# Loading the sorted rows of the expert blocks: two blocks' rows per block in place of a whole stage's rows at once

## The chip, the cores and the metric

One core of a Trainium2 chip runs the kernel. The metric is the device time of one execution in microseconds (us), taken as the median of several runs. A profile of one more execution gives what each engine did and when: PE (TensorE, the matrix products), ACT (ScalarE), DVE (VectorE), POOL (GpSimd), and SP (SyncE), which here does nothing but issue transfers (DMAs).

## The reference

32 sequences of 128 tokens of width 128 pass through gated cross-attention and then through a gated mixture of experts. All in float32. Cut to its core:

```
x = x + tanh(g_xattn) * cross_attention(layernorm(x), ctx)     # 16 heads of 64, 128 keys each
n = layernorm(x)                                               # 4096 tokens x 128
scores = sigmoid(n @ gate_w.T)                                 # 32 experts in 4 groups of 8
group score = sum of the two best (scores + bias) of a group; the best 2 groups stay
the 8 best experts within these two groups; their scores, normalized to 2.5, are the weights w
routed = sum over the 8 experts of w * (silu(n @ gate_e) * (n @ up_e)) @ down_e    # inner size 64
shared = (silu(n @ sg) * (n @ su)) @ sd
out = x + tanh(g_ffn) * (routed + shared)
```

A token only ever needs the experts of its two groups. There are six pairs of groups.

## The kernel before

**Attention.** A loop over the 32 sequences (lines 931 to 1009) holds the attention. It ends some 310 us into the profiled span, and it is the same in both kernels.

**Sorting.** The tokens are dealt into six classes, one for each pair of groups, and written row by row into a table `xs` in DRAM, so that 128 rows in succession are a *block* whose tokens share their pair of groups. A row holds the token's 16 expert weights, its 128 normalized values and its number. This happens in three batches (`choose`, line 513), since the first tokens are through the attention long before the last. Each batch makes a set of blocks known: 7, then 8, then 22 (`SHARE`, line 49), which the code calls stages 0, 1 and 2. Of the 37 blocks, 35 are always worked on (`NSURE`), the last two only if the data need them (line 1350). POOL writes the rows with indirect DMAs (`put`, line 698). When the table of a stage is computed, `ready[k]` is set; `complete(k)` (line 1250) also asks that no row of the stage is still to be written.

**Blocks.** The loop at line 1309 goes over the blocks j. For each of the two groups s of a block, PE multiplies the block's tokens with the gate and up weights of 8 experts (`g` and `u`, 128x512 each), ACT takes the silu of `g` (tile `act`), DVE multiplies `u` by the expert weights (tile `uw`), then `act` by `uw` (tile `h`). PE multiplies `h` with the down weights, and both groups add into `y`. ACT scales it to `o`, and POOL adds `o` to the output rows with an indirect DMA (`finish`, line 1223). Work is issued one half-block ahead: in iteration j stand, in this order, `gate_up(j+1, 0)`, `down(j, 0)`, `gate_up(j+1, 1)` and `down(j, 1)`. `g` and `u` each have two buffers in PSUM, so the product `u` of one half-block can start only once DVE has read `u` of two half-blocks before.

**Two forms of a block.** In a *narrow* block the tokens are on the partitions (`gate_up`, line 1128), and the expert weights are columns of the loaded rows themselves. In a *wide* block (`gate_up_wide`, line 1193) the hidden units are on the partitions, so that `h` needs no turning before the down product; the expert weights of each token must then lie along the free axis, repeated on every partition. That takes a detour over DRAM, begun three blocks ahead:

- `turn_weights` (line 1165): PE turns the block's weights, ACT copies them to `wq` (line 1170) and the tokens to `xT`, and SP stores `wq` to DRAM as `wr` (line 1174).
- `spread_weights` (line 1176): SP loads `wr` back twice, each time repeated on 64 partitions, into the tile `wb` (line 1179). DVE reads `wb` in line 1205.

`wide(j)` (line 1161) holds for blocks 10 to 14 and 17 to 34. Blocks 15 and 16 are narrow.

**Loads of rows.** `load(j)` (line 1098) reads the block's place in `xs` from a table into a register of SP and issues the DMA `xb<-xs` (line 1107), 128 rows of 145 floats. The tile `xb` has 16 buffers. `more_loads(must, may)` (line 1253) is called at the start of every iteration j. It issues all loads up to block `must` (some two or three blocks ahead), and beyond that every load up to block `may` = j + 13 whose stage is complete:

```
more_loads(j + AHEAD if j + AHEAD < NSURE and wide(j + AHEAD) else j + 2, j + 13)
```

**What sets the order.** The order of the work is written out by hand (`tc.manual_schedule()`): each engine, SP among them, takes its instructions in the order of the code. SP's queue thus holds the loads of iteration j ahead of the store and the loads of `wb` that the end of iteration j issues. A DMA that has to wait holds back every later one of SP. When SP has issued eight DMAs, the ninth waits until the first of them has landed, since eight semaphores are used in turn.

Of the kernel before, what the change touches and what calls it, by code (L numbers as in the profile page):

```python
# [39 lines left out]
NSURE = NBLK - 2  # L40
# [14 lines left out]
def gated_cross_attention_moe(  # L55
# [422 lines left out]
    def turn2(pt, c, n):  # L478
        for k in range(n):
            nc.tensor.transpose(pt[:, k * P : (k + 1) * P], rows[:, c + k, NEP:RID], ident)  # L480

    def turned2_out(pt, c, n):
        nc.scalar.copy(x2T[:, c * P : (c + n) * P], pt)

    def logits(pl, c, n):
        for k in range(n):
            nc.tensor.matmul(
                pl[:, k * E : (k + 1) * E], x2T[:, (c + k) * P : (c + k + 1) * P], gw_sb,
                start=True, stop=True,
            )  # L490
# [4 lines left out]
    def logits_out(pl, c, n):  # L495

        k = max(i for i in range(3) if first[i] <= c)
        d = scs[k][:, c - first[k] : c - first[k] + n, :]
        nc.scalar.activation(d, pl.rearrange("p (i e) -> p i e", e=E), AF.Exp, scale=-1.0)

    def logits_done(c, n):
        k = max(i for i in range(3) if first[i] <= c)
        d = scs[k][:, c - first[k] : c - first[k] + n, :]
        v.tensor_scalar(d, d, 1.0, None, ALU.add)
        v.reciprocal(d, d)
# [303 lines left out]
    def gap(room, transfers=1):  # L809

        fresh = True
        while batches and 3 - len(batches) < opened:
            if not piece:
                step_on()
                continue
            w = piece[0]
            if w == "n":
                if not fresh:
                    break
                step_on()  # L820
            elif w in ("pe", "act"):
                break
            else:
                if room <= 0:
                    break
                room -= w
                step_on()
            fresh = False
        put_rows(transfers)
# [6 lines left out]
    def up_products(t, g, u):  # L836
        x_ = x2T[:, t * TT : (t + 1) * TT]
        nc.tensor.matmul(g, sg_sb, x_, start=True, stop=True)
        nc.tensor.matmul(u, su_sb, x_, start=True, stop=True)

    def gated(g, u, a, h):
        nc.scalar.activation(a, g, AF.Silu)
        v.tensor_tensor(h, a, u, ALU.mult)

    def down_products(y, h):
        for i in range(TB):
            nc.tensor.matmul(y[:, i, :], h[:, i * P : (i + 1) * P], sd_sb, start=True, stop=True)
# [3 lines left out]
    def base_out(t, y, o):  # L851
        v.scalar_tensor_tensor(
            out=o, in0=y, scalar=tg2, in1=x_all[:, t * TB : (t + 1) * TB, :],
            op0=ALU.mult, op1=ALU.add,
        )
        w = nc.sync.dma_start(
            out=out_rows[t * TT : (t + 1) * TT, :].rearrange("(i p) d -> p i d", p=P), in_=o
        )
        bases.append(w.ins.name)
# [215 lines left out]
    def small_psum(name):  # L1075
        return ps_t.tile([P, TT], F32, tag="t", name=name)
# [14 lines left out]
    def stage(j):  # L1091
        return max(i for i in range(3) if sum(SHARE[:i]) <= j)

    def psum_place(name):
        place("pe", small_psum(name) if piece and piece[0] == "pe" else None)
        place("act")

    def load(j):
        while not ready[stage(j)]:
            if not piece or piece[0] not in ("pe", "act"):  # L1100
                step_on()
            psum_place(f"pr_{j}")
        while pending and pending[0][0] <= stage(j):
            put_rows(1)
        row, = loaded(mybir.EngineType.SP, j, 0, 1, NROWS - P)
        xbs[j] = m16.tile([P, RW], F32, tag="xb", name=f"xb_{j}")
        reads = [nc.sync.dma_start(out=xbs[j], in_=xs[bass.ds(row, P), :])]
        for r in reads:
            for name in sorts:
                tc.add_manual_dep(  # L1110
                    r.ins, name,
                    mybir.DependencyInfo(mybir.DependencyClass.Sync, mybir.DependencyReason.DATA),
                    reason="the sorted rows",
                )

    def number(j):

        idx[j] = m16.tile([P, 1], I32, tag="idx", name=f"idx_{j}")
        v.tensor_scalar(idx[j], xbs[j][:, RID:], -1.0, float(B * P), ALU.mult, ALU.add)

    def xprep(j):
        pt = small_psum(f"px_{j}")[:, 0:P]
        nc.tensor.transpose(pt, xbs[j][:, NEP:RID], ident)
        xTs[j] = m3.tile([P, P], F32, tag="xT", name=f"xT_{j}")
        nc.scalar.copy(xTs[j], pt)
        groups[j] = loaded(mybir.EngineType.PE, j, 1, 3, NG - 1)
# [34 lines left out]
    def wide(j):  # L1161
        at = j - (NBLK - SHARE[2])
        return -5 <= at < 0 or at >= 2
# [80 lines left out]

    AHEAD = 3
    loaded_ = [0]

    def complete(k):  # L1250
        return ready[k] and not (pending and pending[0][0] <= k)

    def more_loads(must, may):
        while loaded_[0] < NSURE and (
            loaded_[0] <= must or (loaded_[0] <= may and complete(stage(loaded_[0])))
        ):
            load(loaded_[0])
            loaded_[0] += 1

    with tc.manual_schedule():  # L1260
        more_loads(AHEAD, AHEAD)
        hsh = {}

        def up(t):
            g = ps_g.tile([P, TT], F32, tag="g", name=f"sg_{t}")
            u = ps_g.tile([P, TT], F32, tag="u", name=f"su_{t}")
            up_products(t, g, u)
            a = m3.tile([P, TT], F32, tag="act", name=f"sa_{t}")
            hsh[t] = m4.tile([P, TT], F32, tag="h", name=f"sh_{t}")
            gated(g, u, a, hsh[t])  # L1270

        def down_base(t):
            y = ps_y.tile([P, TB, D], F32, tag="y", name=f"sy_{t}")
            down_products(y, hsh.pop(t))
            base_out(t, y, m4.tile([P, TB, D], F32, tag="so", name=f"so_{t}"))

        up(4)
        up(5)
        gap(1.2, 2)
        down_base(4)  # L1280
        psum_place("prs_4")
        gap(1.2, 2)
        up(6)
        pt = small_psum("pt2")
        turn2(pt, 28, 4)
        turned2_out(pt, 28, 4)
        down_base(5)
        gap(1.2, 2)
        pl = small_psum("pl2")[:, 0 : 8 * E]
        logits(pl, 24, 8)  # L1290
        logits_out(pl, 24, 8)
        psum_place("prs_5")
        logits_done(24, 8)
        up(7)
        gap(1.2, 2)
        xprep(0)
        down_base(6)
        psum_place("prs_6")
        gap(1.2, 2)
        opened = 3  # L1300
        gate_up(0, 0)
        xprep(1)
        down_base(7)
        gate_up(0, 1)
        for j in range(AHEAD + 1):
            number(j)
        turned_hidden(0, 0)
        done = -1
        for j in range(NSURE):
            more = j + 1 < NSURE  # L1310
            more_loads(j + AHEAD if j + AHEAD < NSURE and wide(j + AHEAD) else j + 2, j + 13)
            if more:
                (gate_up_wide if wide(j + 1) else gate_up)(j + 1, 0)
            if j + 2 < NSURE and wide(j + 2):
                place_weights(j + 2, 0)
            if done < j - 1:
                finish(j - 1)
                if j - 1 + AHEAD < NSURE:
                    number(j - 1 + AHEAD)
            down(j, 0)  # L1320
            if not wide(j):
                turned_hidden(j, 1)
            if j + 2 < NSURE and not wide(j + 2):
                xprep(j + 2)
            psum_place(f"prb_{j}")
            gap(1.4, 1)
            if more:
                (gate_up_wide if wide(j + 1) else gate_up)(j + 1, 1)
            if j + 2 < NSURE and wide(j + 2):
                place_weights(j + 2, 1)  # L1330
            down(j, 1)
            if not wide(j) or not more:
                finish(j)
                done = j
                if AHEAD < j + AHEAD < NSURE:
                    number(j + AHEAD)
            if more and not wide(j + 1):
                turned_hidden(j + 1, 0)
            if j + AHEAD < NSURE and wide(j + AHEAD):
                turn_weights(j + AHEAD)  # L1340
                spread_weights(j + AHEAD)
            gap(1.4, 2)
# [71 lines left out]
```

## Time and profile before

| | us |
|---|---|
| median of 3 runs | 552.41 (552.32 to 552.97) |
| the profiled execution's own time | 552.61 |
| its span, first to last instruction | 550.8 |
| PE busy | 512.7 (93% of the span) |
| DVE busy | 406.0 (74%) |
| ACT busy | 380.5 (69%) |
| POOL busy | 275.2 (50%) |
| mean granted clock of PE | 0.982 of full speed |

The span is what the trace shows; the own time of the same execution also holds 1.8 us around it. The chain that ended last (the profile follows it back from the last instruction, at each step to what released it) runs 71% over PE, 19% over DVE, 3% over ACT and 2% over DMAs. In a timeline line, the first two numbers are the start and the length of a piece of work in us. A line of the waits gives who waited for what, the sum in us, how many times, and the longest one.

### The profile page before, as it was taken

The numbers are of one execution on the slowest core, as the hardware profiler recorded it, in microseconds if no ns is written. First come the engines' busy times: TensorE is split into PE (matmuls) and PEld (weight loads), VectorE is DVE, ScalarE is ACT, GpSimd is POOL, SyncE is SP. The second block draws the span as 40 slices with busy tenths as digits, with TensorE's granted clock in tenths as the row PEclk, the third lists the DMA queues.
The fourth block names the chain that finished last, engine by engine and source line by source line (L and its number), as shares of the span: only waits on it lengthen the run. The fifth ranks groups of instructions, "written<-read, shape, count | busy, mean of one in ns | idle before, by whom it ended". The sixth has DMA issues, their size and how long they took to land.

```text
span 550.8 us, 15971 instructions
## 1 busy us (share of the span) xinstructions
PE 512.7 (93%) x5942; PEld 448.1 (81%) x5942; DVE 406.0 (74%) x920; ACT 380.5 (69%) x1422; POOL 275.2 (50%) x248
## 2 busy tenths in 40 slices
PE   5899999999999999998999979999996999999992
PEld 4777888988999988897977656676895799999992
DVE  3779999898998899998887877998652455555551
ACT  1688989989899888997882234444772577777760
POOL 5355557566775756864764811743752212232332
PEclk9899999999999999999999979999999999999997
DMA  9994440806213010000001332131555255453541
GB/s 238 226 336 145 151 150 14 289 4 202 99 34 138 2 42 1 2 2 3 2 2 31 97 95 41 38 70 16 122 132 107 51 117 122 104 123 85 129 89 15
DMA packets 50524, 50.49 MB, mean 92 GB/s; under 512 B 20992, under 2 KB 39168, under 8 KB 50064
## 3 DMA queue, kind: packets, MB, share of 16 engines
q1 hardware_dynamic: 43968, 44.38, 28.0%
q0 software_dynamic: 6192, 4.56, 5.8%
q8 instruction: 49, 0.80, 0.6%
q10 hardware_dynamic: 288, 0.52, 0.3%
q14 instruction: 27, 0.22, 0.2%
HBM read 28.06 MB, written 21.58 MB: 90 GB/s over the span
## 4 chain that ended last, share of the span: by engine, by line
PE 71%; DVE 19%; ACT 3%; POOL 2%; DMA 2%; issue 1%; POOLq 0%; SPq 0%; DVEq 0%
PE y L1216 11%; PE o_ps L436 8%; PE s_ps L369 8%; PE g L1199 7%; PE u L1199 7%; PE o_ps L415 7%; PE o_ps L328 6%; DVE nmax L376 5%; DVE eT L404 4%; PE u L1133 4%; PE g L1131 4%; DVE xn L307 3%; PE ph L1152 2%; ACT e L389 2%; DVE oT L424 1%
## 5 line engine op out<-in xcount | busy, mean ns | idle before, releaser
L389 ACT ACTIVATE e<-s_ps,nmax 128x128 f32<-128x128 f32 x512 | 181.6, 384 | 9.6 <-DVE nmax L376 8.2
L398 POOL TENSOR_TENSOR e<-e,rs 128x1024 f32<-128x1024 f32 x64 | 121.4, 1898 | 92.5 <-DVE rs L396 92.5
L1227 POOL DMA_INDIRECT out_dram<-o,idx x35 | 55.8, 1594 | 133.6 <-ACT o L1225 102.8
L389 ACT ACTIVATION_READ_ACCUMULATOR e<-s_ps,nmax 128x1 f32 x512 | 114.0, 223 | 0.0
L376 DVE TENSOR_REDUCE nmax<-s_ps 128x8 f32<-128x1024 f32 x64 | 76.9, 1202 | 11.7 <-PE s_ps L369 11.5
L1205 DVE TENSOR_TENSOR uw<-u,wb 128x512 f32<-128x512 f32 x46 | 31.8, 691 | 67.6 <-PE u L1199 53.7
L404 DVE STREAM_TRANSPOSE eT<-e 128x1024 f32<-128x1024 f32 x64 | 78.7, 1229 | 0.9 <-POOL e L398 0.9
L369 PEld LDWEIGHTS s_ps<-kvT_sb,qT 64*128 64x128 f32 x1024 | 63.8, 191 | 18.7 <-issue 11.1
L369 PE MATMUL s_ps<-kvT_sb,qT 64*128 64x128 f32 x1024 | 76.1, 289 | 3.0 <-ACT e L389 1.9
L436 PE MATMUL o_ps<-c_sb,oT 128*128 128x128 f32 x512 | 65.4, 281 | 6.8 <-DVE oT L424 6.8
L436 PEld LDWEIGHTS o_ps<-c_sb,oT 128*128 128x128 f32 x512 | 59.7, 191 | 13.6 <-DVE oT L424 10.7
L415 PE MATMUL o_ps<-eT,kv 32*64 32x256 f32 x2048 | 66.0, 380 | 2.1 <-DVE c_sb L285 1.0
L328 PE MATMUL o_ps<-xnT,a_sb 128*128 128x128 f32 x480 | 59.8, 278 | 0.0
L328 PEld LDWEIGHTS o_ps<-xnT,a_sb 128*128 128x128 f32 x480 | 56.6, 194 | 0.3 <-issue 0.2
L415 PEld LDWEIGHTS o_ps<-eT,kv 32*64 32x64 f32 x2048 | 49.4, 131 | 8.1 <-DVE c_sb L285 1.4
L1216 PE MATMUL y<-ed_sb,h 128*128 x368 | 49.0, 277 | 0.0
L1199 PE MATMUL u<-xT,wc 128*128 128x128 f32 x368 | 48.6, 275 | 0.0
L1199 PE MATMUL g<-xT,wc 128*128 128x128 f32 x368 | 48.6, 275 | 0.0
L1216 PEld LDWEIGHTS y<-ed_sb,h 128*128 128x128 f32 x368 | 45.6, 195 | 1.5 <-issue 1.0
L1203 ACT ACTIVATE act<-g 128x512 f32<-128x512 f32 x46 | 27.5, 597 | 27.0 <-PE g L1199 27.0
L1199 PEld LDWEIGHTS u<-xT,wc 128*128 128x128 f32 x368 | 44.8, 192 | 0.0
L1199 PEld LDWEIGHTS g<-xT,wc 128*128 128x128 f32 x368 | 44.7, 192 | 0.0
(203 smaller groups left out, 813.7 us busy)
## 6 DMA issues: line engine op xcount, KB each, us to landing
xs<-zero SPq DMA_DIRECT2D x8, 1740.0 KB, 10.3
wb<-wr SPq DMA_DIRECT2D x46, 256.0 KB, 3.7
kv<-in_kv_dram SPq DMA_DIRECT2D x32, 128.0 KB, 4.9
xb<-xs SPq DMA_DIRECT2D x35, 72.5 KB, 2.4
x_all<-in_x_dram SPq DMA_DIRECT2D x8, 256.0 KB
kvT_sb<-in_kvT_dram SPq DMA_DIRECT2D x6, 256.0 KB, 6.0
eg_sb<-in_exp_gT_dram SPq DMA_DIRECT2D x1, 1024.0 KB, 6.9
eu_sb<-in_exp_uT_dram SPq DMA_DIRECT2D x1, 1024.0 KB
```

The source lines that it names most:

```text
L328: nc.tensor.matmul(o_ps[1][:, p // HP, p % HP * P : (p % HP + 1) * P], a_sb[:, p].rearrange("d j k -> d (j k)"), x_, start=True, stop=True,)
L369: nc.tensor.matmul(s_ps[g][:, j, q, :], qT[b][r, g * HP + q, :], kvT_sb[r, b * P : (b + 1) * P], start=True, stop=True,)
L376: v.tensor_reduce(nmax[b, g], s_ps[g].rearrange("p j q k -> p (j q) k"), AX.X, ALU.max, negate=True)
L389: nc.scalar.activation(es[b][:, g, j, q, :], s_ps[g][:, j, q, :], AF.Exp, bias=n[:, c], accum_out=sums[b, g][:, c],)
L398: nc.gpsimd.tensor_tensor(e, e, rs.unsqueeze(2).to_broadcast([P, NP, P]), ALU.mult)
L404: v.transpose(eTs[b][:, g].rearrange("p j q n -> p (j q n)"), es[b][:, g].rearrange("p j q n -> p (j q n)"))
L415: nc.tensor.matmul(o_ps[a // 2][j * KV : (j + 1) * KV, a % 2, 0 : NP * Q].rearrange("k (g q n) -> k g q n", g=2, q=HP), kv_sb[b // TB][r, ...
L436: nc.tensor.matmul(o_ps[0][:, 0, 0:D], o[:, p].rearrange("k a n -> k (a n)"), c_sb[:, p, :], start=(p == 0), stop=(p == NP - 1),)
L1199: nc.tensor.matmul(pt[:, q, :], w[:, k, q * P : (q + 1) * P], xTs[j], start=True, stop=True)
L1205: v.tensor_tensor(uw, u, wbs[j][:, s], ALU.mult)
L1216: nc.tensor.matmul(ys[j], hT[:, q, :], ed_all[:, bass.ds(groups[j][s] * FG + q * D, D)], start=(s == 0 and q == 0), stop=(s == 1 and q == ...
L1227: w = nc.gpsimd.indirect_dma_start(out=out_rows, out_offset=bass.IndirectOffsetOnAxis(ap=idx.pop(j), axis=0), in_=o, in_offset=None, bound ...
```

## The change

`more_loads` gets a third argument `most`: the number of loads that one call may issue while it is ahead of `must`. Loads that `must` asks for are issued as before, but count too. In the loop over the blocks `most` is 2. The call ahead of the loop, which has `must` and `may` both at 3, gets 0.

```
-    def more_loads(must, may):
+    def more_loads(must, may, most):
         while loaded_[0] < NSURE and (
-            loaded_[0] <= must or (loaded_[0] <= may and complete(stage(loaded_[0])))
+            loaded_[0] <= must or (most > 0 and loaded_[0] <= may and complete(stage(loaded_[0])))
         ):
             load(loaded_[0])
             loaded_[0] += 1
+            most -= 1
...
-        more_loads(AHEAD, AHEAD)
+        more_loads(AHEAD, AHEAD, 0)
...
-            more_loads(j + AHEAD if j + AHEAD < NSURE and wide(j + AHEAD) else j + 2, j + 13)
+            more_loads(j + AHEAD if j + AHEAD < NSURE and wide(j + AHEAD) else j + 2, j + 13, 2)
```

## The prediction, made before the result was known

> **What bounds the kernel now.** I read the waits of the whole span first, then the timelines of SP, DVE and PE around the longest wait that reaches PE, then the table of stretches with the granted clock. The waits (who, for what: us in total, times, longest):
>
> ```profile
> DVE uw L1205 <- PE u L1199: 53.7, 42, 1.8
> ...
> DVE uw L1205 <- DMA wb<-wr: 13.9, 3, 10.1
> ...
> PE u L1133 <- DVE uw L1205: 5.2, 1, 5.2
> ```
>
> Most of DVE's waits here are for PE, which is the later of the two. Three times DVE waits for `wb` instead, once for 10.1 us, and once PE then waits for DVE. The waits of PE from 426 us to the end name this one alone. The three stretches from 429 to 540 us show PE busy without a gap, at the full clock; here is one:
>
> ```profile
> 429.00:465.00 36.00, 36.00 (x291) 33.02 (x291) 17.29 (x32) 25.68 (x57) 7.79 (x6) 1.00 0.43 97
> ```
>
> So PE bounds the kernel from 429 us on: what PE gains at 425 us reaches the end, what others gain later does not. Why was `wb` late? SP's timeline:
>
> ```profile
> 403.51 0.31 SPq L1174 DMA_DIRECT2D wr<-wq  x1
> 406.26 1.08 SPq L1179 DMA_DIRECT2D wb<-wr  x2
> 409.11 8.87 SPq L1107 DMA_DIRECT2D xb<-xs  x10
> 418.07 0.38 SPq L1174 DMA_DIRECT2D wr<-wq  x1
> 420.26 1.10 SPq L1179 DMA_DIRECT2D wb<-wr  x2
> 421.92 2.07 SPq L1107 DMA_DIRECT2D xb<-xs  x3
> ```
>
> The ten loads of blocks 15 to 24, stage 2's first burst, stand ahead of block 14's store `wr`. ACT had written its `wq` at 408.81 + 0.26 = 409.07 us (ACT's timeline), yet it goes out at 418.07. DVE and PE pay:
>
> ```profile
> 414.07 0.69 DVE L1207 TENSOR_TENSOR h<-act,uw 128x512 f32<-128x512 f32 x1
> 424.90 0.69 DVE L1205 TENSOR_TENSOR uw<-u,wb 128x512 f32<-128x512 f32 x1 [10.14 <-DMA wb<-wr]
> ```
>
> ```profile
> 414.86 1.06 PE L1199 MATMUL u<-xT,wc 128*128 128x128 f32 x8
> ...
> 419.44 1.02 PE L1131 MATMUL g<-eg_sb,xT 128*128 x2
> 425.65 2.07 PE L1133 MATMUL u<-eu_sb,xT 128*128 x2 [5.19 <-DVE uw L1205]
> 427.52 1.68 PE L1216 MATMUL y<-ed_sb,h 128*128 x8
> 429.03 0.27 PE L1123 MATMUL px<-ident,xb 128*128 128x128 f32 x1
> ```
>
> Block 15's `u` needs the buffer that block 14's `uw` still has to read. After the pause PE is slow for a while:
>
> ```profile
> 425.65:429.10 3.45, 3.45 (x11) 2.41 (x12) 3.19 (x6) 0.00 (x0) 0.00 (x0) 0.54 0.00 1
> ```
>
> The last three numbers are clock, DMA share and GB/s: 0.54 of the full clock.
>
> **What the change moves.** It adds and removes no instruction. I compared the two built programs queue by queue: PE, ACT, DVE and POOL keep the order of their work, and only the semaphores of some DMA waits are renumbered. On SP three things follow.
>
> *Start and stage 1.* Blocks 0 to 14 are loaded in the same order, and nothing stands between the loads of 7 to 14 in either program, so spreading them over four iterations of the code changes nothing: the first `wr` (block 10) comes behind load 14 both times. Cost 0, up to 409 us.
>
> *The burst.* Between the `wb` of block 13 and the `wr` of block 14 there are two loads (15, 16) instead of ten. One load costs SP (8.87 - 0.33) / 9 = 0.95 us. Eight fewer: 7.6 us. `wr` goes out at 418.07 - 7.58 = 410.49 us, and its `wq` is there (409.07). From `wr` to `wb` it took 2.19 us (420.26 - 418.07), and 1.39 (433.15 to 434.54) to 2.75 (403.51 to 406.26) elsewhere; I take 2.19, the same transfer behind the same kind of loads: 412.68. From the issue of `wb` to `uw` it took 4.64 us (424.90 - 420.26); the waits for blocks 12 and 13 ended 4.99 and 4.88 us after theirs (400.39 to 405.38, 406.26 to 411.14), and the shortest landing, 3.4, on the second of the pair, 0.63 later, gives 4.03. I take 4.64: `uw` starts at 417.3, bounds 415.96 to 418.2. (415.96 is when `u` itself is there: 414.86 + 1.10, as in 439.61 to 440.71.)
>
> When would this hold PE? Without the pause block 15's `u` follows its `g` by 0.86 us (429.14 to 430.00): 420.30. `uw` takes 0.69 and the handover 0.06, so `uw` must start by 419.55. The next reader, `y` of block 14 at 421.16, needs `h`, 1.49 us behind the start of `uw`: by 419.67. I have 2.2 us to spare, and 1.3 at the late bound. PE's pause goes; DVE still waits some 1.3 us for `wb`, and that is the next late thing, hidden behind PE.
>
> The sum on PE: start of `u` 425.65 - 420.30 = 5.35; that `u` took 427.52 - 425.65 = 1.87 instead of 0.86, so 1.01; the `y` behind it 429.03 - 427.52 = 1.51 instead of 0.89, so 0.62. Together **6.98 us**.
>
> *The loads that were eight earlier.* Loads 17 to 22 come behind `wb` of block 14, in iterations 12 to 14, where no `wr` stands between: about 414 to 419.5 us, while the next `wr` (block 17) has its `wq` only at 433.1 - 7.0 = 426.1. Cost 0. Then the `wr` of blocks 18 to 22 each have two loads ahead instead of one. In a steady iteration now: `wr` 450.79, `wb` 452.21, load 453.87 + 0.34 = 454.21, next `wr` 456.37. One more load (0.95) ends at 455.16, so 1.2 us stay free; the first of these iterations, with narrow halves, is longer still (433.15 to 439.46). Cost 0. If that cover were gone, `wb` has more: its pair lands by 452.21 + 0.63 + 4.2 (the longest landing) = 457.0, `uw` of that block starts at 457.88, and PE itself would wait only if `uw` were another 4.2 us late (block 17: `uw` 440.71 + 0.75, block 18's `u` 445.63). The rows still arrive blocks ahead: block 17's by 417 us, and they are turned only in iteration 14. The 16 buffers that loads 17 on take were last read in blocks 1 on. POOL's output DMAs follow `o`, which follows PE.
>
> **The sum.** The profiled execution took 552.61 us: 552.61 - 6.98 = 545.63. The median of the runs is 0.20 lower: **545.4 us**, 1.3% less. A difference under 0.2% (1.1 us) cannot be told from no change here.
>
> **The rivals.**
>
> *Part of the pause stays (0.08).* `wr` and `wb` of block 14 now run beside POOL's output DMAs of 412.03 and 416.19 and the loads 15 to 18. Each us by which the two legs exceed 6.83 + 2.2 = 9.1 us is a us of PE. Against it: the longest legs seen sum to 2.75 + 4.99 = 7.7. With 2 us of pause: 547.4. A pause of 3.5 us that brings the slow clock back gives 545.4 + 3.5 + 1.63 = 550.5. (The Trainium skill, "TensorE: Matmul & The Clock Gate", Part 1, says that PE falls to half clock after an idle window of about 3.4 us. By that rule the 2 us pause would cost no clock; no shorter pause in this stage shows it.)
>
> *No gain (0.04).* If moving the issues moved nothing, because `wb` waits for the transfers and not for SP, the time stays 552.4. The row speaks against it: `wr` went out 0.09 us after the tenth load was issued (409.11 + 8.87 = 417.98), not after it landed, which takes 2.4 us more. (The skill, "DMA: Bandwidth & Descriptors", "Issuing engines are not separate DMA queues", calls the time to initiate a DMA usually small relative to the DMA itself. By that rule there would be little to gain; ten issues in 8.87 us with `wr` right behind say otherwise.) That the change does not do what it says belongs here; SP's new order speaks against it.
>
> *Slower (0.05).* Five times (`wr` of blocks 18 to 22) a second load stands ahead of `wr`. It decides if such a load costs SP L > 1.2 + 0.95 = 2.15 us, as it would if it waited for an earlier transfer. Lateness then adds up to 5 x (L - 2.15), of which 0.9 + 4.2 = 5.1 us are covered. If a load waits out the longest landing of one (4.0) and its own 0.95, L is 4.95: 5 x 2.8 - 5.1 = 8.9 us on PE, 545.4 + 8.9 = 554.3. It is slower from L = 4.8 on. Against it: the last three loads of the burst behind `wb` (421.92, 2.07 us for three) wait for nothing.
>
> **How the numbers follow.** Forecast 0.83, the others as given. The range takes the forecast with the spread of the runs (0.65 us downward: 544.7) and the small part of the partial pause (up to 2 us: 547.5). Faster: 0.83 + 0.08 = 0.91; within 0.2%: 0.04; slower: 0.05.
>
> **What would show it.** Right: SP issues two loads, then `wr` near 410.5 and `wb` near 412.7; `uw` waits for `wb` 1 to 3 us instead of 10.1; PE has no wait for `uw` in line 1133 and no stretch near 0.54 clock; the span is 543.8. Wrong: a wait of PE for `uw` in blocks 15 to 23, `uw` waiting for `wb` in blocks 18 to 22, or SP held at line 1107 between two `wb`.

## The result, and the profile after

| | before | after |
|---|---|---|
| median | 552.69 us (552.32 to 555.17, 4 runs) | 544.48 us (543.8 to 547.05, 4 runs) |
| ratio | | 0.9851, 95% interval 0.9807 to 0.9894 |
| the profiled execution's own time | 552.61 | 544.62 |
| its span | 550.8 | 542.8 |
| mean granted clock of PE | 0.982 | 0.987 |

The change is faster by 8.2 us. The forecast was 545.4; the median lies 0.2 us below the lower end of the range (544.7). First the waits of the kernel after (who, for what: us in total, times, longest):

```profile
DVE uw L1205 <- PE u L1199: 38.5, 31, 1.8
...
DVE uw L1205 <- DMA wb<-wr: 23.6, 10, 4.4
```

The longest wait of `uw` for `wb` is 4.4 us instead of 10.1, and PE's wait for `uw` in line 1133 is not in the list any more. There are, however, ten waits for `wb` instead of three; the section on the experiments comes back to them. SP's timeline shows the new order:

```profile
404.84 1.08 SPq L1179 DMA_DIRECT2D wb<-wr  x2
409.34 1.91 SPq L1107 DMA_DIRECT2D xb<-xs  x2
411.31 0.42 SPq L1174 DMA_DIRECT2D wr<-wq  x1
413.08 1.09 SPq L1179 DMA_DIRECT2D wb<-wr  x2
414.70 5.22 SPq L1107 DMA_DIRECT2D xb<-xs  x6
```

Two loads, then the store of block 14 at 411.31 instead of 418.07; loads 17 to 22 follow behind its `wb`. On DVE and on PE:

```profile
418.14 0.69 DVE L1205 TENSOR_TENSOR uw<-u,wb 128x512 f32<-128x512 f32 x1 [4.37 <-DMA wb<-wr]
```

```profile
418.44 1.02 PE L1131 MATMUL g<-eg_sb,xT 128*128 x2
419.30 1.02 PE L1133 MATMUL u<-eu_sb,xT 128*128 x2
420.16 1.05 PE L1216 MATMUL y<-ed_sb,h 128*128 x8
421.05 0.27 PE L1123 MATMUL px<-ident,xb 128*128 128x128 f32 x1
```

`u` follows `g` by 0.86 us, and `y` and `px` come at their full-speed distances. From this `g` to this `px` it took 2.61 us; before it took 9.59 (419.44 to 429.03). The difference is 6.98 us, the sum of the prediction to the last digit: the sum was read from this same profile before, and what remained to be seen was that nothing of the pause stays. But `g` itself starts 1.00 us earlier than before, and nothing that the change moves lies ahead of it. In this pair of profiles that microsecond fits the granted clock 90 us earlier, after PE's pause at 320 us, where it waits for the first row loads: there the kernel after is still 0.47 us later than before (323.60 against 323.13, the first product of block 0), and on the way to `g` it wins back 1.5, with 3.4 us less at half clock (at most 1.7 us of work). In the stretches from 320 to 325 us and from 325 to 330 us (third number from the end: clock) the kernel before shows

```profile
320.00:325.00 5.00, 1.94 (x7) 1.29 (x7) 3.51 (x16) 1.20 (x3) 0.00 (x0) 0.80 0.26 60
325.00:330.00 5.00, 5.00 (x14) 2.83 (x14) 2.98 (x14) 0.86 (x2) 0.00 (x0) 0.52 0.56 159
```

and the kernel after

```profile
320.00:325.00 5.00, 1.89 (x7) 0.93 (x6) 4.09 (x17) 1.77 (x3) 0.00 (x0) 0.91 0.25 59
325.00:330.00 5.00, 5.00 (x21) 3.44 (x21) 3.28 (x15) 0.86 (x2) 0.00 (x0) 0.75 0.62 172
```

At half clock a stretch of 5 us with a mean of 0.80 has 2.0 us of it and one with 0.52 has 4.8: 6.8 us before, and 0.9 + 2.5 = 3.4 us after. From 330 us on the clock is 1.00 in both. So there is one theory for each part: for the 7 us the place of `wr` and `wb` in SP's queue, against the traffic of ten loads at once; for the remaining microsecond luck of the clock, against an effect of the change that the prediction did not see.

### The profile page after: what moved, and what is told of

Its sections match the earlier page's. It is cut to its first block, busy times and chain, and to the rows that moved or that the text cites. A ratio compares the mean times of both kernels' runs of the same rounds, so it can differ in the third digit from the quotient of the medians.

```text
span 542.8 us, 15971 instructions
## 1 busy us (share of the span) xinstructions
PE 509.8 (94%) x5942; PEld 447.1 (82%) x5942; DVE 405.7 (75%) x920; ACT 380.5 (70%) x1422; POOL 275.6 (51%) x248
## 4 chain that ended last, share of the span: by engine, by line
PE 72%; DVE 20%; ACT 3%; POOL 2%; issue 1%; DMA 1%; POOLq 0%; DVEq 0%
PE y L1216 11%; PE o_ps L436 8%; PE u L1199 8%; PE g L1199 8%; PE s_ps L369 8%; PE o_ps L415 7%; PE o_ps L328 6%; DVE nmax L376 5%; DVE eT L404 4%; PE g L1131 4%; PE u L1133 4%; DVE xn L307 3%; PE ph L1152 2%; ACT e L389 2%; DVE oT L424 1%
## 5 line engine op out<-in xcount | busy, mean ns | idle before, releaser
L1227 POOL DMA_INDIRECT out_dram<-o,idx x35 | 56.2, 1607 | 124.7 <-ACT o L1225 91.2
```

What stands on the lines that cost most here:

```text
L1227: w = nc.gpsimd.indirect_dma_start(out=out_rows, out_offset=bass.IndirectOffsetOnAxis(ap=idx.pop(j), axis=0), in_=o, in_offset=None, bound ...
```

## The experiments

Since the time ahead of block 15 differs between executions, I read each trace by its *tail*, the span less the start of the first `g` of block 15 (419.44 before, 418.44 after). *Lead* is the time from the issue of load 15 to that `g`, *reach* the time from the issue of load 15 to `uw` of block 14. The pause is what the start of `u` loses against 0.86 us behind `g`. All in us; the last column is the ratio to the kernel before on the same chip with its 95% interval.

| kernel, loads ahead of `wr` | reach | lead | pause | tail | ratio |
|---|---|---|---|---|---|
| before, 10 | 15.79 | 10.33 | 5.35 | 131.4 | |
| before again, 10 | 15.45 | 11.38 | 3.96 | 130.2 | 1.0026 (0.9999 to 1.0053) |
| eight per block, 8 | 13.50 | 11.32 | 2.07 | 126.8 | 0.9939 (0.9911 to 0.9967) |
| six per block, 6 | 11.52 | 11.34 | 0.06 | 124.7 | 0.9896 (0.9863 to 0.9929) |
| four per block, 4 | 9.66 | 9.89 | 0 | 124.4 | 0.9858 (0.9805 to 0.9911) |
| after, 2 | 8.80 | 9.10 | 0 | 124.4 | 0.9851 (0.9807 to 0.9894) |
| after again, 2 | 8.12 | 10.20 | 0 | 124.4 | 0.9846 (0.9812 to 0.9881) |
| after, third, 2 | 10.14 | 11.29 | 0 | 124.4 | 0.9876 (0.9836 to 0.9915) |
| one per block, 1 | 8.73 | 10.36 | 0 | 124.4 | 0.9895 (0.9859 to 0.9932) |
| two, then the rest, 2 | 8.51 | 9.97 | 0 | 124.4 | 0.9858 (0.9827 to 0.989) |
| weights by POOL, 10 in SP's queue | 9.52 | 9.82 | 0 | 124.7 | 0.9893 (0.9856 to 0.9931) |
| burst behind, 0 | | | 0 | 124.4 | 0.9894 (0.9861 to 0.9927) |

**The kernel before again**, unchanged.

> The kernel before once more, unchanged. The first g of block 15 started at 419.44 us in the profile before and at 418.44 in the profile after, ahead of all that the change moves; the stretch from 320 to 330 us had the clock at half for 6.8 us before and for 3.4 us after. Theory 'luck of the clock': how long the clock stays low after PE's pause at 320 us differs from one execution to the next, whatever the kernel; then this run may show either 3.4 or 6.8 us, and runs of one kernel differ by up to 1.7 us. Rival 'the change did it': this run shows 6.8 us and a start at 419.4 again, and all its times lie within 552.3 to 553.0. Ratio to the kernel before 1.000 by both.

The clock was never low from 320 to 335 us in this trace: 0 us, against 6.8 in the first profile of the same kernel. So how long it is low is luck, and the rival falls. But `g` starts at 419.24, hardly earlier than in the first profile, so the clock alone does not set it. The stretch from the first product of block 0 to this `g` took 96.31 us in the first profile (6.8 us low) and 94.91 here (0 us low); in the changed kernel it took 94.84 in the first profile (3.4 us low), 96.91 and 94.79 in the two later ones (3.4 and 0 us low). What else moves it is open. Medians were 555.04 us (551.18 to 558.15, 10 runs) beside 553.57 for the 24 runs of the kernel before (549.75 to 557.68): executions of one kernel lie as much as 8 us apart, where the three runs known before the prediction lay 0.65 apart. The pause is here too, in PE's timeline:

```profile
419.24 1.02 PE L1131 MATMUL g<-eg_sb,xT 128*128 x2
424.06 1.12 PE L1133 MATMUL u<-eu_sb,xT 128*128 x2 [3.79 <-DVE uw L1205]
425.02 1.47 PE L1216 MATMUL y<-ed_sb,h 128*128 x8
426.28 0.42 PE L1123 MATMUL px<-ident,xb 128*128 128x128 f32 x1
```

It is shorter by 1.4 us: load 15 went out earlier ahead of `g` (lead 11.38 instead of 10.33; here it did not wait for POOL's rows, where it waited 1.0 us in the first profile), and the ten loads with what follows took 0.34 us less. The clock falls after it as well, but only some 1.4 us after PE is back: from 425 to 426 us its mean is still 0.75, so half clock began near 425.5. From 426 to 429.5 us:

```profile
426.00:429.50 3.50, 3.50 (x9) 1.77 (x8) 1.61 (x4) 0.86 (x2) 0.00 (x0) 0.58 0.02 5
```

**Four loads per block.** The edit to the changed kernel: `j + 13, 2)` becomes `j + 13, 4)`.

> The changed kernel with four loads per block in place of two, so four loads (15 to 18) stand ahead of the store wr of block 14. Theory 'queue of SP': each further load holds wr back by 0.95 us. In the changed kernel uw of block 14 started at 418.14, and PE is held once it starts after 418.55; two loads more give 420.04, so PE pauses about 1.5 us in line 1133, too short for the clock to fall: 544.5 + 1.5 = 546.0. Rival 'transfers': wb was late because ten loads moved 725 KB at once on the same DMA engines; four loads are few, so PE does not pause: 544.5.

No pause, median 546.28. By the queue of SP there should have been 1.5 us, so the number missed; the reason stands in the table. Reach 9.66 is 0.9 longer than with two loads, where 1.9 was expected, and the lead was 0.8 longer. With so few loads other things set the reach too: it is 8.12 to 10.14 in the four traces with two loads, and in the longest of them `wr` waited 0.8 us for ACT and took 3.13 us to `wb`. This trace alone does not tell the theories apart.

**Six loads per block.** `j + 13, 2)` becomes `j + 13, 6)`.

> The changed kernel with six loads per block: six loads (15 to 20) ahead of wr of block 14. Queue of SP: four loads more than in the changed kernel, 3.8 us; uw of block 14 at about 421.9, PE pauses about 3.4 us: 547.9, or 549.5 if the clock falls to half after it as it did after the pause of 5.2 us. Transfers: six loads of 72.5 KB are still under half of what wb itself moves; a pause of 1 us at most: 544.5 to 545.5.

A pause of 0.06 us, where 3.4 was expected; median 547.24 (545.75 to 552.02). Reach grew to 11.52, but the lead was 11.34. Both traces came out as 'transfers' had it, but a *lead* that covers six loads says little about how much a load costs. (Six loads move 435 KB, which is not under half of the 512 KB that the two loads of `wb` move.) Eight loads can tell.

**Eight loads per block.** `j + 13, 2)` becomes `j + 13, 8)`.

> The changed kernel with eight loads per block, so loads 15 to 22 stand ahead of the wr of block 14. In the traces so far load 15 goes out 9.1 to 11.4 us ahead of the first g of block 15, depending on when POOL's last rows have landed; PE is held when uw of block 14 starts later than g + 0.11. Queue of SP: with two loads uw started 8.8 us after load 15 went out; six more at 0.95 make 14.5, so PE pauses 3.0 to 5.3 us, and the tail is 124.4 + 3 to 5.3, and up to 1.7 more if the clock falls: 127.4 to 131.4. Rival 'eight in flight': SP may have eight DMAs under way, so loads cost only once there are more than that; no pause, tail 124.4.

SP's and PE's timelines:

```profile
408.12 6.92 SPq L1107 DMA_DIRECT2D xb<-xs  x8
415.13 0.38 SPq L1174 DMA_DIRECT2D wr<-wq  x1
```

```profile
419.44 1.02 PE L1131 MATMUL g<-eg_sb,xT 128*128 x2
422.37 1.12 PE L1133 MATMUL u<-eu_sb,xT 128*128 x2 [1.91 <-DVE uw L1205]
```

There is a pause, 2.07 us, so 'eight in flight' falls. It is below the 3.0 expected, since the reach was 13.50, not 14.5. With it the traces obey one sum: pause = reach - lead - 0.11 gives 5.35, 3.96, 2.07 and 0.07 for ten, ten, eight and six loads, against 5.35, 3.96, 2.07 and 0.06 read from PE. That sum says that PE waits for this `uw` and for nothing else; what tells the theories apart is how the reach grows. From four to ten loads the reach grows by (15.6 - 9.66) / 6 = 0.99 us per load, close to the 0.95 of SP's queue. The median is 552.31, faster than before by 0.6%, against 1.5% with two. The profiled execution is the fastest of its ten (547.97). The pause cost no clock:

```profile
425.00:429.00 4.00, 4.00 (x21) 2.61 (x20) 2.31 (x5) 1.66 (x5) 0.00 (x0) 1.00 0.01 4
```

**The burst kept in SP's queue, `wr` and `wb` of block 14 issued by POOL.** The edits to the kernel before:

```
-        nc.sync.dma_start(out=wrows[j]...
+        (nc.gpsimd if j == 14 else nc.sync).dma_start(out=wrows[j]...
...
-            nc.sync.dma_start(out=wbs[j]...
+            (nc.gpsimd if j == 14 else nc.sync).dma_start(out=wbs[j]...
```

> The kernel before with its ten loads ahead in SP's queue, but wr and wb of block 14 alone are issued by POOL, which is idle then. Queue of SP: they no longer stand behind the loads; PE does not pause in line 1133, tail 124.4, though the ten loads move at the same time. Transfers: the ten loads crowd the DMA engines as before, wb lands late and PE pauses 3 to 5 us: tail 128 to 131.

SP and POOL, from the timeline (SP's piece ends with the timeline's stretch):

```profile
410.70 6.16 SPq L1107 DMA_DIRECT2D xb<-xs  x7
411.03 0.60 POOL L1174 DMA_DIRECT2D wr<-wq  x1
414.55 1.08 POOL L1179 DMA_DIRECT2D wb<-wr  x2 [2.93 <-DMA wr<-wq]
```

All ten loads go out as before, and move while `wr` and `wb` do; PE does not pause, tail 124.7. So the order in SP's queue is the cause. Reach against lead left PE 0.4 us, so the traffic alone did not hold PE here. That it slows `wr` is not shown: from the issue of `wr` to that of `wb` it took 3.52 us (411.03 to 414.55), but block 13's took 3.40 us in the trace with eight loads (401.73 to 405.13), ahead of the burst.

**The burst of ten behind `wr` and `wb`.** The edits to the kernel before:

```
-            more_loads(j + AHEAD if j + AHEAD < NSURE and wide(j + AHEAD) else j + 2, j + 13)
+            must = j + AHEAD if j + AHEAD < NSURE and wide(j + AHEAD) else j + 2
+            more_loads(must, must if j == 11 else j + 13)
...
                 spread_weights(j + AHEAD)
+            if j == 11:
+                more_loads(must, j + 13)
```

> The kernel before, but in iteration 11 the ten loads of blocks 15 to 24 are issued, all together, behind the wr and wb of block 14 instead of ahead of them. Queue of SP: wr no longer waits for any load; PE does not pause, and uw of block 14 waits less for wb than the 4.4 us of the changed kernel; the wb of blocks 21 to 26 are no longer late either (one load or none ahead of each wr); 544.5 as with the change. Transfers: the ten loads now run beside the landing of wb of block 14 and crowd it as before: PE pauses for some us, 548 to 552.

Line 1133 has no pause, but now load 15 is the late one, one step ahead of the tail:

```profile
418.57 0.33 PE L1123 MATMUL px<-ident,xb 128*128 128x128 f32 x1 [0.90 <-DMA xb<-xs]
```

Load 15 went out at 415.58 only. With the 0.49 us that PE then waits for `xT`, the next `g` starts 2.78 us behind the `y` ahead of it (416.62 to 419.40), where it is 1.00 us in the kernel after (414.76 to 415.76): this takes back 1.8 us; median 547.58. What the queue holds ahead of `wr` has to be the loads that are needed first, and no others.

**Two loads ahead, the other eight behind, all at once.** As the kernel just shown, with `more_loads(must, 16 if j == 11 else j + 13)`.

> The kernel before, but in iteration 11 only loads 15 and 16 go ahead of the wr and wb of block 14, and the other eight follow behind them all together. Queue of SP: that is all the change does for PE: tail 124.4, no pause in line 1133, no wait of PE for load 15 (as there was with all ten behind); same ratio as the changed kernel, 0.985 to 0.989. Rival 'the spreading over the blocks counts': eight loads in a row beside the landing of wb, and behind it, cost PE something: tail over 125.5.

Tail 124.4, no pause, no wait for load 15; median 546.06 (544.04 to 548.11). `uw` waits for `wb` once (3.2 us) in the whole rest. So the change's gain is this one exchange of order in iteration 11; that later loads are spread gains nothing.

**One load per block.** `j + 13, 2)` becomes `j + 13, 1 if j >= 11 else 2)`.

> The changed kernel with one load per block from iteration 11 on (two before that). One load ahead of the wr of block 14, and one ahead of each later one. Queue of SP: PE was not held with two, so nothing is gained: tail 124.4; but the seven waits of uw for wb from 456 to 489 us in the changed kernel (1.6 to 2.8 us each) go, since the second load ahead of wr made them. Rival 'spreading helps by itself': the fewer loads the better, tail under 124. If the seven waits stay, the second load is not their cause.

The tail is 124.4, but the waits of `uw` did not go: 14 of them behind block 14 (from 457.8 to 530 us), 33.5 us in all. So the second load is not their cause, and my theory of them falls. They are not the change's work at all, as far as these traces go: behind block 14 the kernel before has none in its first trace and three in its second (491 to 502 us), the changed kernel seven, two and six, the kernel with six loads none. The tail is 124.4 with two of them as with fourteen. They begin with a `wr` that lands late. SP's timeline, block 21:

```profile
449.51 0.34 SPq L1174 DMA_DIRECT2D wr<-wq  x1
453.08 1.09 SPq L1179 DMA_DIRECT2D wb<-wr  x2
```

Here 3.57 us pass instead of 1.41 as in the kernel before (456.37 to 457.78); in the kernel after it was 448.39 to 451.70 at the same block, and in the second trace of the kernel before 482.82 to 486.28, at block 26. From then on each `wr` goes out earlier behind the `wb` of the block before than it did, and takes 2.4 to 3.8 us to `wb`. Why these were slow is open.

**The changed kernel, again and a third time**, unchanged.

> The changed kernel once more, unchanged. To leave out what differs ahead of the change, I read the tail: the span less the start of the first g of block 15. It was 131.4 us in the profile before, 130.2 in the second one of that kernel, and 124.4 after. Luck of the clock: the tail is 124.4 again to 0.2, while g itself starts anywhere from 418 to 422, with 0, 3.4 or 6.8 us of low clock near 330 us. Rival 'the change did it': g starts near 418.4 again, a microsecond ahead of the kernel before, with 3.4 us of low clock.

Tail 124.4; `g` started at 423.72, and the clock was low for 3.4 us. That `g` falls anywhere is confirmed, and so is the tail.

> The changed kernel a third time, with more runs. By the tails (131.4 and 130.2 before, 124.4 twice after) the change is worth 5.8 to 7.0 us, 1.05 to 1.26%; the two medians so far say 1.5%, each with an interval of some 0.4% either way. If the tails tell all, the ratio is 0.987 to 0.989 and its interval holds these; if the change also helps ahead of block 15, which no trace shows, it stays at 0.985 with an interval that leaves 0.987 out.

Tail 124.4, ratio 0.9876, interval 0.9836 to 0.9915. It holds 0.987, as do the two intervals before; none of the three shows more gain than the tails do. By the medians, though, the gain is 8.2, 7.6 and 7.8 us, each time above the 5.8 to 7.0 of the tails. Only two executions of the kernel before were profiled, and the second was the fastest of its ten (551.18, median 555.04), so its tail need not be a usual one. An effect ahead of block 15 is not shown: in the two traces without low clock, one of each kernel, the stretch from block 0's first product to this `g` took 94.91 us before and 94.79 after. A gain of a few tenths of a per cent beyond the tails is not ruled out.

## Why the prediction was right, and where it failed

- *What bounds, and the chain `wr`, `wb`, `uw`, PE:* right, and shown from two sides: `wr` taken out of SP's queue (weights by POOL) and loads added ahead of it (six, eight).
- *6.98 us:* right. That it holds to the last digit only means that it was read from this same profile before and that nothing of the pause stayed. Over several executions the term is no constant: 131.4 - 124.4 = 7.0 and 130.2 - 124.4 = 5.8 us in the two traces of the kernel before.
- *2.2 us to spare:* mis-sized; it was 0.4 (`uw` at 418.14, held from 418.55). From `wr` to `uw` it took 6.83, as taken, but by luck: its two legs were 1.77 and 5.06, not 2.19 and 4.64. And load 15 went out 1.23 us later against PE, since POOL's rows landed later (SP's wait for them was 2.6 us, not 1.0), and the two loads held `wr` 0.6 us longer than taken. So `uw` started 3.2 us behind the moment at which `u` was there (414.96), not 1.3. In the two later traces of the changed kernel 2.2 and 1.3 us were to spare; none of the three paused.
- *Cost 0 for the second load ahead of each later `wr`:* right. `uw` waited for `wb` in blocks 21 to 27, up to 2.8 us, which the prediction had named a sign of being wrong (for blocks 18 to 22). But such waits come without the second load too, and in the kernel before, and PE lost nothing by them.
- *Where it failed:* the range, in the step "the forecast with the spread of the runs (0.65 us downward: 544.7)". Three runs were taken for the whole spread, and the stretch ahead of block 15 was taken to be as long in the next execution as in this one. The 62 runs of the kernel before that are known now lie between 549.75 and 558.35 us; from 552.41 the spread downward is 2.7 us, not 0.65. The profiled pair shows 1.0 us of it, ahead of block 15, where the change does nothing; only in part is its cause known. By 549.75 - 6.98 = 542.8 the lower edge should have gone to 543 or below, with the same forecast. That the first median fell below the edge is chance as well: the three medians of the changed kernel, 544.48, 547.73 and 545.93, lie on both sides of 545.4.
- *The clock:* the Trainium skill, "TensorE: Matmul & The Clock Gate", Part 1, was weighed for a pause of 2 us, which by its window of 3.4 us should cost no clock. The trace with eight loads agrees: 1.9 us idle, clock 1.00. The pauses at 320 us do not: at 2.7 us (kernel before), 2.6 (after) and 1.6 (four loads) they were followed by 6.8, 3.4 and 3.4 us at half clock, so a pause shorter than the window is not safe. The pauses of 3.8 and 5.2 us were each followed by one stretch of half clock, which cost 5.8 - 3.96 = 1.8 and 7.0 - 5.35 = 1.6 us.
- *Issue time:* the Trainium skill, "DMA: Bandwidth & Descriptors", "Issuing engines are not separate DMA queues", has it that the time to initiate a DMA is usually small relative to the DMA itself. Here a load costs SP 0.95 us to issue and 2.4 to land, and ten in a row decided.

## What to carry to other kernels

A queue that issues DMAs is work in order like any engine: before prefetching in one go, ask which dependent store or load of the next block stands behind the burst, and put only the loads needed first ahead of it. Read such a stall from the queue's own timeline (when was the source ready, when did the DMA go out), and size it by reach and lead, in more than one trace, rather than by one trace's pause. Three runs that agree to 0.1% do not give the spread of a kernel.

## What the runs showed of the hardware that was not expected

- PE's pause of 2.7 us at 320 us was followed by 6.8 us at half clock in one execution of the kernel before; one of 1.7 us by none, and in the kernel after one of 2.6 us by 3.4. With four loads one of 1.6 us was followed by 3.4 us, with eight one of 2.1 us by none: the length alone does not decide. Where the clock was low near 320 us, it was so for 3.4 us or for 6.8.
- Half clock need not begin at the pause: after the pause that ended at 424.06 it began near 425.5, some 1.4 us later, with PE busy.
- An 8 KB store that mostly let the next DMA go after 1.4 us took up to 3.8 (`wr` to `wb`, one load per block), and stayed slow for blocks on end; in the kernel before it happened too.
